# A circular filter over eight tiles folded twice instead of once, in a transformer kernel on one core

## The chip, the cores and the metric

The kernel runs on one core of a Trainium2 chip. Its time is the device time of one execution in microseconds (us), the median of several. The engines are called as the profile calls them: PE is the matmul engine (PEld its weight loads), DVE the vector engine, ACT the scalar engine, POOL the GpSimd engine, SP the queue that issues DMAs.

## The reference

The input is x, float32, 2 batches x 1024 positions x 512 features. Four blocks follow each other, each added to x after a layer norm:

```python
x = x + attn_a(layernorm(x))   # differential attention, 16 heads, causal
x = x + ffn(layernorm(x))      # 8 experts of width 16, the best 2 of them
x = x + attn_b(layernorm(x))   # linear attention with rotary embedding
x = x + ffn(layernorm(x))
```

What matters here is the end of attn_a. Each head gives two causal softmax results, f1 and f2, of the same values. Their difference is filtered along the positions:

```python
attn_freq = (rfft(attn1, axis=1) - lambda_full * rfft(attn2, axis=1)) * filt
attn = irfft(attn_freq, n=1024, axis=1)
attn = attn * rsqrt(mean(attn**2, axis=-1) + eps) * rms_weight * (1 - LAMBDA_INIT)
return attn.reshape(bsz, 1024, 512) @ Wout
```

A fixed factor per frequency is a circular convolution over the 1024 positions. With the positions cut into 8 tiles of 128, output tile i is the sum over j of block[(i - j) mod 8] @ tile j, with eight fixed 128x128 matrices.

attn_b applies a rotary embedding (rope) to the left half of q and of k, sums normalised k times v over the positions, and multiplies q by that sum ahead of W_out.

## The kernel before

**The fold.** A circular convolution over 8 blocks splits into one over 4 blocks of the sums of tiles four apart, and a skew one over 4 blocks of their differences. The kernel stores the 4 sums and 4 differences of a batch in `folded[b]` (8 tiles of 128x512). Four matmuls on the sums give the common part of two output tiles, four on the differences give what separates them; the two tiles are common plus and minus that. TILE (L30) therefore orders the tiles so that the two of a pair follow each other, and that order is the order of the work in stage 2. `filt` holds 11 matrices (L66 to L68), loaded by one DMA.

**Stage 1** is the attention of attn_a: 16 units (batch, quarter of the heads, half of a quarter), each with 9 phases, in one loop of steps (L791). A step handles three phases at once: scores (PE, L461) and exponentials (ACT, L492) of phase `now`, the difference of the two softmax results of phase `last`, and the transposes (L551) of phase `old`. Before the exponentials DVE finds the row minima (L475, L483). The difference is made from a ratio per row: `share` multiplies on POOL (L512), `divide` takes a reciprocal on DVE (L518) and multiplies on POOL (L520), and `join` (L527) on DVE applies the ratio to the 128x1024 weights. The order on PE, DVE, ACT and POOL is written by hand: instructions stand on each engine in program order, and lists named front, small, large, middle, final and rear hang extra work on numbered steps.

At the end of a unit `finish` writes the result, 128 x 8 x 64, on DVE (L607), and `fold` (L615 to L627) makes its sums and differences on POOL: three pairs of an addition and a subtraction, one pair over two tiles and two pairs over one, so two operations of 128 elements a partition and four of 64. It hangs on `rear`, so on POOL it lies between one step's divide and the next step's share. `rotate` (L372, L373) and the scaling of the layer norm are POOL's other work in this stage.

In the last two units the first four tiles of batch 0 (MIXED = 4) are filtered within stage 1. `mix_filter` does eight matmuls 128x256 (L701) for a pair of tiles and half of the columns, `mix_part` (L717) adds and subtracts on POOL, `mix_square` (L721, POOL), `mix_sum` (L725, DVE), `mix_tables` (ACT) and `mix_scale` (POOL) normalise, and `mix_turn` (L742) and `mix_project` (L751) transpose and multiply by Wout. FILTER and TURN say at which step k of the last two units each is done. Wout is scaled by rms_weight on POOL (L816) at k = 11, ahead of that step's share.

**Stage 2** runs over t = 0 to 17, one tile a step for each piece of work, each piece some steps behind the one before. In step t, in the order of the code: `filtered` for the products of tile t + 1 (PE L930, a copy on ACT L939 for the first tile of a pair, a subtraction and an addition on DVE, L941 and L942, for the second), `mixed` (transposes of yn), `head_norm` (square on ACT L947, sum on DVE L949, a reciprocal root by Ln and Exp on ACT L97 and L98 with a step on DVE L103 to L106, and yn on DVE L953), `up` (the experts' second matmul added to x, L1104), `attn_norm` (hn_b on DVE L1125, and three POOL operations on 128x512, L1129 to L1131), `attn_qk` for k and later for q (a bias on DVE L1163, then `rope`), `expert_gate`, `attn_v`, `attn_add`, `projected` and `expert_norm`. From t = 12, when nothing more is to be filtered, `up` and `attn_norm` follow `attn_qk`. From t = 10 the rest of attn_b and the last expert block follow.

`rope` writes two intermediates: ra on DVE (L1148), half of rb on DVE (L1149) and the other half on POOL (L1150), and POOL adds the two (L1151). ra and rb come from a pool with two buffers, one for k and one for q of a tile. In this stage the order is written by hand for PE, DVE and ACT; POOL works in program order.

Of the kernel before, what the change touches and what calls it, by code (L numbers as in the profile page):

```python
# [11 lines left out]
F32 = mybir.dt.float32  # L12
# [6 lines left out]
P = 128  # L19
NB, T, E = 2, 1024, 512  # L20
# [6 lines left out]
NE, NI = 8, 16  # L27
MIXED = 4

TILE = [b * JT + k + h for b in range(NB) for k in range(JT // 2) for h in (0, JT // 2)]  # L30
LAMBDA_INIT = 0.8 - 0.6 * math.exp(-0.3 * 12)
EPS = 1e-5
NEG = -1e30
# [2 lines left out]
def constants():  # L36

    f = np.float32
    t = np.arange(T, dtype=f)

    def tiled(a):
        return np.ascontiguousarray(a.reshape(JT, P, -1).transpose(1, 0, 2).reshape(P, -1))

    inv = (f(1.0) / np.power(f(10000.0), np.arange(0, HD, 2, dtype=f) / f(HD))).astype(f)
    fr = np.outer(t, inv).astype(f)


    r = np.arange(P)
    part = np.where(r // 2 % 2, f(1.0), f(-(HD**-0.5)))[:, None]
    sign = np.where(r % 2, f(1.0), f(-1.0))[:, None]  # L50
    rope_a = np.concatenate([part * np.cos(fr).T[r // 4 % 8], part * sign * np.sin(fr).T[r // 4 % 8]], axis=1).astype(f)

    rot = E // 2
    inv = (f(1.0) / np.power(f(10000.0), np.arange(0, rot, 2, dtype=f) / f(rot))).astype(f)
    fr = (t[:, None] * inv[None, :]).astype(f)
    rope_b = np.concatenate([tiled(np.cos(fr)), tiled(np.sin(fr))], axis=1).astype(f)

    x = np.linspace(0.0, 1.0, T // 2 + 1)  # L60
    taps = np.fft.irfft(np.exp(-0.5 * (x / 0.15) ** 2), n=T)
    lag = (128 * np.arange(JT)[None, :, None] + np.arange(P)[None, None, :] - np.arange(P)[:, None, None]) % T


    block = [taps[lag[:, d]] for d in range(JT)]
    halves = [(block[d] + block[d + 4]) / 2 for d in range(4)]  # L66
    halves += [(block[d % JT] - block[(d + 4) % JT]) / 2 for d in range(-3, 4)]
    filt_k = np.concatenate(halves, axis=1).astype(f)  # L68


    tri = np.tile(np.tril(np.ones((NE, NE), f), -1).reshape(1, -1), (P, 1))
    return {"c_rope_a": rope_a, "c_rope_b": rope_b, "c_filt": filt_k, "c_tri": tri}
# [3 lines left out]
def hybrid_layer_kernel(ctx: ExitStack, tc: tile.TileContext, i: dict, out: bass.AP):  # L76
# [50 lines left out]

    PLACE = [2, 7, 6, 5, 4, 3, 1, 0]

    FOLDED = [0, 1, 2]  # L130
    AT = [0, 1, 3, 2]
    late = ctx.enter_context(ExitStack())
    with ExitStack() as sa:
        keep = sa.enter_context(tc.tile_pool(name="keep", bufs=1))

        folded = [keep.tile([P, JT, E], F32, tag=f"folded{b}", name=f"folded_{b}") for b in range(NB)]
        wrms = keep.tile([P, 1], F32, tag="wrms", name="wrms")
        filt = keep.tile([P, 11, P], F32, tag="filt", name="filt_sb")
        neg_lam = keep.tile([P, 1], F32, tag="neg_lam", name="neg_lam")

        with ExitStack() as sp:
# [65 lines left out]
            def load_others(k):  # L207
                if k == 0:
                    for k in range(4):
                        nc.sync.dma_start(wrms[32 * k : 32 * k + 32, :], i["rms_weight"].rearrange("(p o) -> p o", o=1))  # L210
                elif k == 1:
                    nc.sync.dma_start(wdr, i["w_dr"].rearrange("(c p) f -> p c f", p=P))
                elif k == 2:
                    nc.sync.dma_start(wup, i["w_up"])
                    nc.sync.dma_start(filt, i["c_filt"].rearrange("p (d q) -> p d q", d=11))
                else:
                    nc.vector.tensor_scalar_mul(wrms, wrms, 1.0 - LAMBDA_INIT)

# [396 lines left out]
            def fold(n):  # L615

                b, qt, blk = units[n]
                col = 32 * (4 * qt + 2 * blk)
                r = results.pop(n)

                for to, (low, high, w) in ((2, (5, 0, 2)), (1, (7, 3, 1)), (0, (2, 4, 1))):
                    for op, s in ((nc.gpsimd.tensor_add, 0), (nc.gpsimd.tensor_sub, 4)):
                        op(  # L623
                            folded[b][:, FOLDED[to] + s : FOLDED[to] + s + w, col : col + 64],
                            r[:, low : low + w, :],
                            r[:, high : high + w, :],
                        )  # L627

# [4 lines left out]
            def at(which, t, what, *args):  # L635
                which.setdefault(t, []).append((what, args))
# [54 lines left out]

            mix = {}

            def mix_filter(bank, c0, k, half):
                cols = slice(256 * half, 256 * half + 256)
                y = bank[:, c0 : c0 + 512]
                for d in range(2):
                    for j in range(4):  # L700
                        nc.tensor.matmul(  # L701
                            y[:, 256 * d : 256 * d + 256],
                            filt[:, 4 + k - j + 3 if d else (k - j) % 4, :],
                            folded[0][:, 4 * d + AT[j], cols],
                            start=(j == 0),
                            stop=(j == 3),
                        )
                yield
                sd = mix["sd"] = work.tile([P, 2, 256], F32, tag="sd", name=f"sd_{k}_{half}")
                nc.scalar.copy(sd, y.rearrange("p (d f) -> p d f", d=2))  # L710

            def mix_part(k, half):
                sd = mix.pop("sd")
                for n, op in ((2 * k, nc.gpsimd.tensor_add), (2 * k + 1, nc.gpsimd.tensor_sub)):
                    if half == 0:
                        mix["y", n] = mixy.tile([P, E], F32, tag="y", name=f"y_a{n}", bufs=4)
                    op(mix["y", n][:, 256 * half : 256 * half + 256], sd[:, 0, :], sd[:, 1, :])  # L717

            def mix_square(n):
                sq = mix["sq", n] = work.tile([P, E], F32, tag="sq", name=f"ysq_{n}", bufs=1)  # L720
                nc.gpsimd.tensor_mul(sq, mix["y", n], mix["y", n])  # L721

            def mix_sum(n):
# [31 lines left out]


            FILTER = [5, 8, 9, 10]
            TURN = [13, 14, 17, 18]
            t = (NU - 2) * NP
            for k in range(MIXED // 2):  # L760
                for half in range(2):
                    f = t + FILTER[2 * k + half]
                    at(large, f, mix_filter, 512, k, half)
                    at(middle, f + 1, mix_part, k, half)
                for n in range(2 * k, 2 * k + 2):
                    at(middle, f + 1 + n % 2, mix_square, n)
                    at(rear, f + 2 + n % 2, mix_sum, n)
                    at(front, f + 3 + n % 2, mix_tables, n)
                    at(rear, f + 3 + n % 2, mix_scale, n)
                    at(small, t + TURN[n], mix_turn, n, misc if TURN[n] < 2 * NP else spare)  # L770
                    at(large, t + TURN[n], mix_project, 512, n)

            ordered = {mybir.EngineType.PE, mybir.EngineType.DVE, mybir.EngineType.Activation}
            with tc.manual_schedule(engines=ordered | {mybir.EngineType.Pool}):
# [92 lines left out]
        with ExitStack() as sb:  # L867
# [52 lines left out]

            ys, yns, yTs = {}, {}, {}

            def filtered(n):


                d = n % 2
                b, q = divmod(n // 2, JT // 2)
                y = wide(f"y_{n}")
                for k in range(4):
                    nc.tensor.matmul(  # L930
                        y,
                        filt[:, 4 + q - k + 3 if d else (q - k) % 4, :],
                        folded[b][:, 4 * d + AT[k], :],
                        start=(k == 0),
                        stop=(k == 3),
                    )
                ys[n] = w2k(f"y_{n}", "y", bufs=3)
                if d == 0:
                    nc.scalar.copy(ys[n], y)  # L939
                else:  # L940
                    nc.vector.tensor_sub(ys[n], ys[n - 1], y)  # L941
                    nc.vector.tensor_add(ys[n - 1], ys[n - 1], y)  # L942

            def head_norm(n):
                y = ys.pop(n)
# [195 lines left out]
            def rope(t, j, key):  # L1141
# [2 lines left out]
                cos = rope_b[:, 0, j, :, None].to_broadcast([P, E // 4, 2])  # L1144
                sin = rope_b[:, 1, j, :]
                ra = work.tile([P, E // 4, 2], F32, tag="ra", name=f"ra_{key}")
                rb = work.tile([P, E // 4, 2], F32, tag="rb", name=f"rb_{key}")
                nc.vector.tensor_mul(ra, left, cos)  # L1148
                nc.vector.scalar_tensor_tensor(rb[:, :, 0], left[:, :, 1], -1.0, sin, ALU.mult, ALU.mult)  # L1149
                nc.gpsimd.tensor_mul(rb[:, :, 1], left[:, :, 0], sin)  # L1150
# [69 lines left out]
            with tc.manual_schedule(engines=ordered):  # L1220
                for t in range(NTILE + 2):
# [8 lines left out]
                    if mixing:  # L1230
                        due(expert_back, t - 1, 0, listed=True)
                        if t == 0:
# [4 lines left out]
                            for n in range(2):  # L1237
                                expert_hidden([n], 0)
                            expert_gate([0], 0)

                        for n in range(t + 1 if t else 0, min(t + 2, NTILE - MIXED)):
                            filtered(MIXED + n)
                    turned = MIXED + t - 2 if 0 <= t - 2 < NTILE - MIXED else None
                    if turned is not None:
                        mixed(turned)
                    if 1 <= t <= NTILE - MIXED:
                        head_norm(MIXED + t - 1)
                    if mixing:
                        due(up, t - 1, 0, listed=True)
                        due(attn_norm, t - 1)  # L1250
# [125 lines left out]
```

## Time and profile before

| what | value |
|---|---|
| median of three executions | 1186.89 us (1185.26 to 1187.04) |
| the profiled execution | 1188.05 us |
| its span on the core | 1186.3 us |
| mean granted PE clock | 0.979 |
| stage 1, stage 2 | about 0 to 741 us, 741 to 1186 us |
| PE, DVE, ACT, POOL busy | 1083.5, 950.5, 754.7, 449.0 us |
| fold on POOL (L623) | 96 operations, 1.97 to 1.98 us per unit |
| products of the filter in stage 2 (PE L930) | 96 records for 48 matmuls, 592 ns each |
| products of the filter in stage 1 (PE L701) | 64 records for 32 matmuls, 379 ns each |

Times in the views are microseconds from the start of the span. A line of a timeline or of the chain gives a start, a duration, the engine, the source line and the tile; `x4` says that four instructions are put together. In square brackets stands how long the engine was idle before the instruction, and what ended that. The chain of work that ended last goes back from the last instruction, at each step to what released it. A float32 matmul has two records; records that follow each other overlap, so the time of one is read from a run of them.

### The profile page before, as it was taken

The numbers are of one execution on the slowest core, as the hardware profiler recorded it, in microseconds if no ns is written. First come the engines' busy times: TensorE is split into PE (matmuls) and PEld (weight loads), VectorE is DVE, ScalarE is ACT, GpSimd is POOL, SyncE is SP. The second block draws the span as 40 slices with busy tenths as digits, with TensorE's granted clock in tenths as the row PEclk, the third lists the DMA queues.
The fourth block names the chain that finished last, engine by engine and source line by source line (L and its number), as shares of the span: only waits on it lengthen the run. The fifth ranks groups of instructions, "written<-read, shape, count | busy, mean of one in ns | idle before, by whom it ended". The sixth has DMA issues, their size and how long they took to land.

```text
span 1186.3 us, 23544 instructions
## 1 busy us (share of the span) xinstructions
PE 1083.5 (91%) x8736; PEld 745.6 (63%) x8736; DVE 950.5 (80%) x2025; ACT 754.7 (64%) x1996; POOL 449.0 (38%) x644
## 2 busy tenths in 40 slices
PE   6799999999899999999999977699999989988997
PEld 5577777777677787777777745345454545454554
DVE  4699999989888988998998876578788767747576
ACT  3588988989888888889888855233434332332433
POOL 2335444543433534353354451125344325323300
PEclk9999999999999999999999979799999999989999
DMA  6411211201310110111011602100000000000002
GB/s 208 148 36 56 59 37 51 59 28 41 117 41 15 37 42 15 37 46 37 19 38 41 254 1 86 59 0 1 1 1 0 1 1 1 0 1 36 1 19 88
DMA packets 33346, 52.12 MB, mean 44 GB/s; under 512 B 6481, under 2 KB 11089, under 8 KB 33105
## 3 DMA queue, kind: packets, MB, share of 16 engines
q1 hardware_dynamic: 33232, 50.63, 13.3%
q8 instruction: 69, 1.13, 0.4%
q14 instruction: 45, 0.36, 0.1%
HBM read 23.35 MB, written 6.29 MB: 25 GB/s over the span
## 4 chain that ended last, share of the span: by engine, by line
PE 44%; DVE 32%; ACT 13%; issue 5%; POOL 5%; DMA 1%; SPq 1%; DVEq 0%; POOLq 0%; ACTq 0%
ACT p L492 8%; PE s L461 8%; DVE p L527 7%; DVE least L483 6%; PE bank L329 5%; PE dtp L551 4%; PE py L1215 4%; PE bank L578 3%; PE pq_q L1156 2%; DVE least L475 2%; POOL folded L623 2%; PE hr_f L1031 2%; PE pq_k L1156 2%; PE pq_v L1156 2%; PE y L930 2%
## 5 line engine op out<-in xcount | busy, mean ns | idle before, releaser
L492 ACT ACTIVATE p<-s,least 128x640 f32<-128x640 f32 (+7 forms) x512 | 377.9, 744 | 40.4 <-DVE least L483 24.4
L483 DVE TENSOR_REDUCE least<-s 128x1 f32<-128x896 f32 (+5 forms) x384 | 244.1, 680 | 34.7 <-PE s L461 34.7
L527 DVE SCALAR_TENSOR_TENSOR p<-p,ratio,p 128x1024 f32<-128x1024 f32 (+7 forms) x256 | 233.1, 946 | 9.8 <-POOL ratio L520 8.7
L551 PE MATMUL dtp<-ident,p 128*128 128x128 f32 x1152 | 186.0, 285 | 20.6 <-DVE p L527 9.8
L553 ACT COPY dt<-dtp 128x512 f32<-128x512 f32 x288 | 168.8, 586 | 46.5 <-PE dtp L551 42.9
L461 PE MATMUL s<-keys,qk 32*128 32x128 f32 (+3 forms) x1408 | 169.9, 447 | 3.4 <-DMA keys<-qk 3.4
L551 PEld LDWEIGHTS dtp<-ident,p 128*128 128x128 f32 x1152 | 129.7, 143 | 65.2 <-ACT dt L553 28.1
L475 DVE TENSOR_REDUCE least<-s 128x1 f32<-128x1024 f32 (+1 forms) x96 | 115.8, 1213 | 28.4 <-PE s L461 28.4
L461 PEld LDWEIGHTS s<-keys,qk 32*128 32x128 f32 x1408 | 94.6, 188 | 56.4 <-issue 49.9
L329 PE MATMUL bank<-xnT,wqk 128*128 128x256 f32 x472 | 115.9, 389 | 2.7 <-ACT raw L340 1.8
L520 POOL TENSOR_TENSOR ratio<-ratio,inverse 128x2 f32<-128x2 f32 (+1 forms) x144 | 27.9, 194 | 224.8 <-DVE inverse L518 220.0
L461 PE MATMUL s<-swapped 32*128 32x128 f32 (+2 forms) x896 | 105.6, 347 | 0.0
L512 POOL TENSOR_TENSOR ratio<-sums,neg_lam 128x2 f32<-128x2 f32 (+1 forms) x144 | 69.2, 481 | 95.6 <-ACT p L492 95.6
L492 ACT ACTIVATION_READ_ACCUMULATOR p<-s,least 128x1 f32 x512 | 104.4, 204 | 0.0
L329 PEld LDWEIGHTS bank<-xnT,wqk 128*128 128x128 f32 x472 | 86.1, 193 | 17.6 <-ACT raw L340 5.3
L1129 POOL TENSOR_SCALAR xb_b<-x_sb,mv_b,rr_b 128x512 f32<-128x512 f32 x16 | 37.5, 2343 | 116.2 <-DVE rr_b L106 116.2
L448 PE MATMUL s<-eye 128*128 128x256 bf16 (+1 forms) x320 | 60.9, 251 | 20.2 <-ACT p L492 19.6
L461 PEld LDWEIGHTS s<-swapped 32*128 32x128 f32 x896 | 71.9, 186 | 9.4 <-issue 0.2
L578 PE MATMUL bank<-dt,v 128*32 128x128 f32 x2304 | 69.5, 274 | 0.1
L578 PEld LDWEIGHTS bank<-dt,v 128*32 128x32 f32 x2304 | 60.9, 110 | 5.5 <-issue 3.5
L373 POOL TENSOR_TENSOR other<-other,rope_a_sb 128x512 f32<-128x512 f32 x31 | 64.4, 2076 | 0.0
L1053 ACT ACTIVATE gw_f<-gw_f 128x8 f32<-128x8 f32 (+2 forms) x23 | 4.9, 212 | 93.2 <-DVE gw_f L1049 93.2
(205 smaller groups left out, 1865.7 us busy)
## 6 DMA issues: line engine op xcount, KB each, us to landing
other<-raw SPq DMA_DIRECT2D x64, 128.0 KB, 2.1
xin<-in_query SPq DMA_DIRECT2D x16, 256.0 KB, 2.9
keys<-qk SPq DMA_DIRECT2D x64, 64.0 KB, 1.9
swapped<-qk SPq DMA_DIRECT2D x32, 128.0 KB, 2.3
swapped<-keys SPq DMA_DIRECT2D x32, 128.0 KB, 2.5
x_sb<-in_query SPq DMA_DIRECT2D x16, 256.0 KB, 6.5
out_dram<-x_sb SPq DMA_DIRECT2D x16, 256.0 KB, 2.1
wqk<-in_w_qk SPq DMA_DIRECT2D x8, 256.0 KB, 4.7
```

Of the source, the lines that this page charges most:

```text
L329: nc.tensor.matmul(pp, wqk[:, part, c, :], xnT[b, half][:, c, t0 : t0 + 256], start=(c == 0), stop=(c == EC - 1),)
L373: engine.tensor_mul(other, other, rope_a[:, 1, cols])
L461: nc.tensor.matmul(s[mm][:, c0 : c0 + w], q[r0 : r0 + 32, j * P - back : (j + 1) * P - back], k[r0 : r0 + 32, s0 - back : s0 - back + w], ...
L475: nc.vector.tensor_reduce(least[n][:, e[0] : e[-1] + 1 : e[-1] - e[0] or 1, mm], s[mm].rearrange("p (g k) -> p g k", g=g), AX.X, ALU.min,)
L483: nc.vector.tensor_reduce(least[n][:, e, mm : mm + 1], s[mm][:, c0 : c0 + w], AX.X, ALU.min)
L492: nc.scalar.activation(ps[mm][:, c0 : c0 + w], sv, AF.Exp, bias=low, scale=-1.0, accum_out=sums[n][mm][:, e : e + 1],)
L512: nc.gpsimd.tensor_mul(ratio[:, w], first, neg_lam.to_broadcast([P, w.stop]))
L527: nc.vector.scalar_tensor_tensor(ps[0][:, c0 : c0 + w], ps[1][:, c0 : c0 + w], ratio[:, k : k + 1], ps[0][:, c0 : c0 + w], ALU.mult, ALU.add,)
L551: nc.tensor.transpose(tp[:, k * P : (k + 1) * P], d[:, c0 : c0 + P], ident)
L553: nc.scalar.copy(dt[:, 4 * half : 4 * half + 4, :], tp.rearrange("p (k q) -> p k q", k=4))
L578: nc.tensor.matmul(po[32 * g : 32 * g + 32, c0 : c0 + P], vals[n // 2 % 2][:, k, 64 * (n % 2) + 32 * h : 64 * (n % 2) + 32 * h + 32], dt[: ...
L1156: nc.tensor.matmul(pq, hTs[n][:, c, :], win(c, s), start=(c == 0), stop=(c == EC - 1))
```

## The change

The circular part of the filter is folded again. The sums of tiles four apart are themselves split into sums and differences (tiles two apart), so their part is two products of two matmuls each; the differences of the first fold stay as they were, four matmuls per product. Four output tiles now come from 2 + 2 + 4 + 4 = 12 matmuls where there were 16, in three stages of additions and subtractions. TILE orders the tiles in fours, and `filt` has 12 matrices.

`fold` makes the three subtractions as before, writes the sums in place over `result`, and adds and subtracts these once more: four operations of 128 elements and four of 64. In stage 1 `mix_filter` and `mix_part` work by kind (common or apart) and half, for four tiles at once; the later steps of a tile go by `f + 1 + n // 2`, and TURN is 14, 17, 18, 19. `sd` and `ysq` share a tag with two buffers. In stage 2 `common` and `apart` take the place of `filtered`: products at t = 0 (twice), 1, 3, 4, 5, 7, 8 and 9; the buffers for y are four. `head_norm` stands ahead of them and of `mixed`. In `rope`, rb has one buffer.

```diff
-TILE = [b * JT + k + h for b in range(NB) for k in range(JT // 2) for h in (0, JT // 2)]
+TILE = [b * JT + q + k for b in range(NB) for q in range(2) for k in (0, 4, 2, 6)]
...
+    def sum_products(q, d):
+        if d == 0:
+            return [((q - k) % 2, 1 - k) for k in range(2)]
+        return [(3 + q - k, 3 - k) for k in range(2)]
+
+    def difference_products(q):
+        return [(8 + q - k, 4 + AT[k]) for k in range(4)]
...
-                for to, (low, high, w) in ((2, (5, 0, 2)), (1, (7, 3, 1)), (0, (2, 4, 1))):
-                    for op, s in ((nc.gpsimd.tensor_add, 0), (nc.gpsimd.tensor_sub, 4)):
-                        op(
-                            folded[b][:, FOLDED[to] + s : FOLDED[to] + s + w, col : col + 64],
-                            r[:, low : low + w, :],
-                            r[:, high : high + w, :],
-                        )
+                to = folded[b][:, :, col : col + 64]
+                for k, (low, high, w) in ((2, (5, 0, 2)), (0, (7, 3, 1)), (1, (2, 4, 1))):
+                    r0, r1 = r[:, low : low + w, :], r[:, high : high + w, :]
+                    nc.gpsimd.tensor_sub(to[:, 4 + k : 4 + k + w, :], r0, r1)
+                    nc.gpsimd.tensor_add(r1, r0, r1)
+                nc.gpsimd.tensor_add(to[:, 0:2, :], r[:, 3:5, :], r[:, 0:2, :])
+                nc.gpsimd.tensor_sub(to[:, 2:4, :], r[:, 3:5, :], r[:, 0:2, :])
...
-            def mix_part(k, half):
+            def mix_part(q, half, kind):
                 sd = mix.pop("sd")
...
+                if kind == 0:
+                    nc.gpsimd.tensor_add(y[0], sd[:, 0, :], sd[:, 1, :])
+                    nc.gpsimd.tensor_sub(y[2], sd[:, 0, :], sd[:, 1, :])
+                else:
+                    for d in range(2):
+                        nc.gpsimd.tensor_sub(y[2 * d + 1], y[2 * d], sd[:, d, :])
+                        nc.gpsimd.tensor_add(y[2 * d], y[2 * d], sd[:, d, :])
...
-            TURN = [13, 14, 17, 18]
+            TURN = [14, 17, 18, 19]
...
-            def filtered(n):
...
+            def common(n):
+                b, q = divmod(n // 4, 2)
+                ab = [wide(f"y_{n}_{d}") for d in range(2)]
+                for d in range(2):
+                    products(ab[d], sum_products(q, d), b)
+                for k in (0, 2):
+                    ys[n + k] = w2k(f"y_{n + k}", "y", bufs=4)
+                nc.scalar.copy(ys[n], ab[0])
+                nc.vector.tensor_sub(ys[n + 2], ys[n], ab[1])
+                nc.vector.tensor_add(ys[n], ys[n], ab[1])
+
+            def apart(n):
+                b, q = divmod(n // 4, 2)
+                y = wide(f"y_{n}_2")
+                products(y, difference_products(q + n % 4), b)
+                ys[n + 1] = w2k(f"y_{n + 1}", "y", bufs=4)
+                nc.vector.tensor_sub(ys[n + 1], ys[n], y)
+                nc.vector.tensor_add(ys[n], ys[n], y)
...
-                rb = work.tile([P, E // 4, 2], F32, tag="rb", name=f"rb_{key}")
+                rb = work.tile([P, E // 4, 2], F32, tag="rb", name=f"rb_{key}", bufs=1)
...
-                        for n in range(t + 1 if t else 0, min(t + 2, NTILE - MIXED)):
-                            filtered(MIXED + n)
+                    if 1 <= t <= NTILE - MIXED:
+                        head_norm(MIXED + t - 1)
+                    if mixing:
+                        n = MIXED + t
+                        if t == 0:
+                            common(n)
+                        if t % 4 == 0:
+                            apart(n)
+                        elif t % 4 == 1:
+                            apart(n + 1)
+                        elif t % 4 == 3 and n + 1 < NTILE:
+                            common(n + 1)
                     turned = MIXED + t - 2 if 0 <= t - 2 < NTILE - MIXED else None
                     if turned is not None:
                         mixed(turned)
-                    if 1 <= t <= NTILE - MIXED:
-                        head_norm(MIXED + t - 1)
```

## The prediction

> **What bounds the kernel now.** I read the page's busy row first, then the chain that ended last, first over the span and then in two windows, and then the timelines of the engines that those windows name.
>
> ```profile
> span 1186.3 us, 23544 instructions
> PE 1083.5 (91%) x8736; PEld 745.6 (63%) x8736; DVE 950.5 (80%) x2025; ACT 754.7 (64%) x1996; POOL 449.0 (38%) x644
> ...
> PE 44%; DVE 32%; ACT 13%; issue 5%; POOL 5%; DMA 1%; SPq 1%; DVEq 0%; POOLq 0%; ACTq 0%
> ```
>
> PE is busy for 91% but holds only 44% of the chain, so work taken from PE counts only in the stretches where PE sets the end. POOL, busy 38%, has 5% of the chain, and most of that is the fold. The chain where a unit's fold runs (one of 14 such places):
>
> ```profile
> 606.00 0.50 DVE result L607
> ...
> 606.58 1.24 POOL folded L623 x4
> ...
> 607.95 0.59 POOL folded L623 x2
> 608.55 0.15 POOL ratio L512
> ...
> 608.78 0.20 POOL ratio L520
> ...
> 609.00 3.42 DVE p L527 x2
> ...
> 613.65 1.46 ACT p L492 x4
> ```
>
> The second ratio waits for POOL's queue; the join (L527) starts 0.02 after it, and DVE's minima had ended at 608.95, so nothing else holds the join. In each of the folds of units 0 to 13 the timeline shows this order, with the ratio's end 0.02 to 0.03 after the last minimum and the join right behind. Stage 2, t = 6, DVE's timeline and then POOL's:
>
> ```profile
> 868.13 0.43 DVE L1148 TENSOR_TENSOR ra_q<-qkv_q,rope_b_sb 128x256 f32<-128x256 f32 x1
> 868.47 1.36 DVE L1149 SCALAR_TENSOR_TENSOR rb_q<-qkv_q,rope_b_sb 128x128 f32<-128x128 f32 x1
> 869.75 0.28 DVE L1047 TENSOR_SCALAR sg_f<-hr_f 128x128 f32<-128x128 f32 x1
> ```
> ```profile
> 865.83 2.35 POOL L1129 TENSOR_SCALAR xb_b<-x_sb,mv_b,rr_b 128x512 f32<-128x512 f32 x1 [8.46 <-DVE rr_b L106]
> 868.26 1.42 POOL L1130 TENSOR_TENSOR xb_b<-xb_b,bout_sb 128x512 f32<-128x512 f32 x1
> 869.76 1.27 POOL L1131 TENSOR_TENSOR x_sb<-x_sb,xb_b 128x512 f32<-128x512 f32 x1
> 870.99 0.48 POOL L1150 TENSOR_TENSOR rb_k<-qkv_k,rope_b_sb 128x128 f32<-128x128 f32 x1
> 871.54 0.72 POOL L1151 TENSOR_TENSOR qkv_k<-ra_k,rb_k 128x256 f32<-128x256 f32 x1
> ```
>
> POOL finishes the k rope (872.26) long after DVE wants to begin rb_q (868.47). The chain has rb_q as DVE's link at 826.28, 846.76, 868.55, 889.03, 910.81 and 931.28: from t = 4 to t = 10 DVE sets the step. Its yn (L953) begins at 840.31, 862.11, 882.58, 904.36, 924.83, 946.62: 21.78 us in a step with a y pair (L941, L942), 20.47 in one without. PE's own work is 20.9 a step (773.44 to 794.26 and on to 815.07, the starts of tp_y in the chain), so DVE leads only narrowly; up to t = 3, and again from about 955, PE sets the end.
>
> **The folds.** Six POOL operations of a unit become eight: 2 of 128 elements and 4 of 64 become 4 and 4. By start times in POOL's instructions, a 128-element one takes 0.410 and a 64-element one 0.278 until the next starts (2 x 0.410 + 4 x 0.278 = 1.93; the row of six shows 1.97). New: 4 x 0.410 + 4 x 0.278 = 2.75, so +0.82. [...]
> The three sums now go in place into result, which the subtraction before them reads, and the first of the last two operations reads those sums: the changed kernel's instruction list shows four waits of POOL on itself per fold, and none inside a fold before. The trace has such waits: L1130 begins at 868.26, 0.08 after L1129 ends (868.18), and L1131 0.08 after L1130 (869.68), while fold operations start 0.045 before their predecessor's end. So a wait costs 0.08 + 0.045 = 0.12, four cost 0.48. Bounds: 0 (the wait already met) to 0.58. I take 0.48: **+1.30 a unit**. Behind it in POOL's queue are both ratios, behind those the join, then the next minima, exponentials and scores; the window's edges are all tight, so nothing gives it back. 14 x 1.30 = **+18.2** (11.5 to 19.6). Unit 15's fold (737.8) is followed by no POOL work until 761 and unit 14's is counted with the tail.
>
> **The filter of the first four tiles (stage 1's end).** Matmuls 128x256 fall from 32 to 24, 16 records (8 matmuls) lasting 3.6; PE saves 1.8 at k = 5 and at k = 9 of that tail. mix_part grows from 8 to 12 POOL operations of 0.685 each (+2.7), the squares, sums and scalings of tiles 0 and 1 move a step or so earlier and tile by tile, and the turns and projections go from k = 13, 14, 17, 18 to 14, 17, 18, 19. The place that decides is here:
>
> ```profile
> 687.06 1.72 DVE L527 SCALAR_TENSOR_TENSOR p<-p,ratio,p 128x1024 f32<-128x1024 f32 x1 [4.95 <-POOL ratio L520]
> ```
> ```profile
> 678.02 1.04 POOL L721 TENSOR_TENSOR ysq<-y_a 128x512 f32<-128x512 f32 x1 [2.66 <-DVE yms L725]
> 679.01 1.42 POOL L717 TENSOR_TENSOR y_a<-sd 128x256 f32<-128x256 f32 x2
> 680.41 6.19 POOL L816 TENSOR_SCALAR wout_sb<-wout_sb,wrms 128x512 f32<-128x512 f32 x4
> ```
>
> The scaling of wout stands ahead of the share and the join waits 4.95. With mix_part no longer behind a square that waits 2.66 for DVE, wout starts near 675.7, the join near 682.4: a lead of 4.6. It is spent again: the fold of unit 14 (1.3), later squares, and at k = 19 one turn and projection (3.5 to 3.9 of PE) that now precede weigh and finish. Net **-0.8** (-4 to +3).
>
> **Stage 2's products.** 48 matmuls 128x512 become 36: four, 3.44 us, go at t = 2, 6 and 10. ACT loses three copies of 0.58, DVE gets three more y pairs, of 1.30 to 1.32 (t = 0 twice, then 1, 3, 4, 5, 7, 8, 9, in place of 0, 2, 4, 6, 8, 10). head_norm goes ahead of them on ACT and DVE; its wait for r_m (0.53) stays. At t = 1 the norm need not wait for that step's products, which starts t = 2 about 1 earlier. With the matmuls gone at t = 2, hn_b comes some 5.5 earlier, in the part that PE set.
> At t = 2 and t = 6 PE idles longer. [...] Here PE idled 3.74 ahead of 767.91 and the next eight records took 5.08 instead of 3.45: +1.6. [...]
>
> **rope's rb.** The pool gets one buffer for rb instead of two. So rb_q on DVE waits for POOL's addition that reads rb_k. At t = 6 that is free at 872.26, and rb_q would begin 3.7 after its present start. It then takes about 0.3 in place of 1.36, as it no longer runs beside xb (rb_k at 867.21 took 0.28): the end moves by 2.7. Behind it on DVE stand the gate's operations; the six from ranks to gate take 2.26 beside POOL now (871.17 to 873.43) and took 1.25 at 745.60 with POOL idle, so 1.0 returns. **+1.8 a step** (1.0 to 2.7). In steps from t = 12 POOL is free by then (999.41 to 1000.13 against rb_q at 1000.34); at t = 10 and 11 PE's work covers it.
> Sum: 5.5 less 1.8 at t = 2 leaves a lead of 3.7 to 3.8; sq's wait gone at t = 3 gives 0.6; two more y pairs in t = 3 to 9 than before cost 2.65; seven stalls cost 12.6. Net **+11** (5 to 16). DVE steps are then 22.3 and 23.6, PE's 20.9 or 17.4: PE's saving at t = 6 lies behind DVE.
>
> **Sum.** 18.2 - 0.8 + 11 = 28.4; the profiled execution took 1188.05 (span 1186.3, and 1.75 around it) and would take 1216.4. The median, 1186.89, lies 1.16 lower: **1215 us**.
>
> **Rivals.**
> 1. Faster: PE sets the end and POOL's waits are covered. What is removed counts in full: 12 x 0.86 + 8 x 0.45 = 13.9, giving 1173. For it: PE 91% busy. Against it: the join's start 0.02 after the ratio, and DVE's chain of t = 4 to 10. It decides if a fold adds under 1.0 (14 x 1.0 = 13.9) and rb_q is not held. Chance 0.03.
> 2. The folds cost as said, but rb_q's wait is covered. Stage 2 then gains: -3.8 - 1.8 - 0.6 + 2.65 is -3.5 at most; PE's own 20.9 a step leaves about -2.7. 18.2 - 0.8 - 2.7 = 14.7, giving 1201.6. It needs POOL's chain to end 3.7 sooner. Chance 0.10.
> 3. POOL's waits on itself are free: 11.5 in place of 18.2, giving 1208.5. Chance 0.15.
> 4. All costs at their upper ends: 2.7 a stall (+6.3), half of the clock's 3.3, folds 19.6: giving about 1225. Chance 0.12.
> 5. Gains and losses cancel within 0.2% (what a measurement of this kernel can tell from no change): chance 0.01.
> The forecast itself: 0.59.
>
> **How the numbers follow.** 1215 is the likeliest. The lower ends of all terms (11.5 - 4 + 5) give 1199, the upper ends 1225; cases 2 to 4 and the forecast lie within 1200 to 1226, which keeps room for 2 in 10 outside. Faster 0.03, same 0.01, slower 0.96.
>
> **What would show it.** In the profile after: fold groups of eight with some 3.2 us from the first start to the next ratio, and joins still right behind the ratio (else the first term is wrong); no idle near 5 before the join at k = 11; DVE idle of 3.6 ahead of rb_q, put down to POOL's qkv_k, in t = 2 to 9, and yn spaced 22 to 24. Wrong would be: short waits of POOL on itself, rb_q starting at once, or a join that waits for something other than the ratio.

## The result, and the profile after

The changed kernel takes 1229.91 us (median of four, 1228.99 to 1232.63) against 1186.97 us before: a ratio of 1.0363, with a 95% interval of 1.0336 to 1.0390. That is 43 us more, where 28 were forecast. The profiled execution took 1228.99, its span is 1227.1, and 40.8 us of span are to be placed.

The page of the changed kernel:

```profile
span 1227.1 us, 23506 instructions
PE 1091.0 (89%) x8696; PEld 750.1 (61%) x8696; DVE 939.1 (77%) x2031; ACT 751.6 (61%) x1993; POOL 471.4 (38%) x680
...
PE 38%; DVE 33%; ACT 12%; POOL 9%; issue 6%; DMA 1%; SPq 0%; POOLq 0%; DVEq 0%; ACTq 0%
```

PE has 20 matmuls less to do and is busy for 7.5 us longer: its mean granted clock went from 0.979 to 0.961. POOL's part of the chain went from 5% to 9%.

The simplest way to place the time is to take an instruction that both traces have and to subtract its starts. The table does that for the first operation of a fold and for later marks.

| mark | before | after | shift |
|---|---|---|---|
| fold of unit 0 | 102.36 | 102.38 | +0.0 |
| fold of unit 13 | 647.71 | 664.25 | +16.5 |
| the join's ratio at k = 11 of the tail | 686.84 | 701.10 | +14.3 |
| fold of unit 14 | 697.37 | 712.38 | +15.0 |
| fold of unit 15, the end of stage 1 | 737.76 | 763.34 | +25.6 |
| yn of t = 2 | 777.18 | 797.25 | +20.1 |
| yn of t = 10 | 946.62 | 981.97 | +35.4 |
| yn of t = 12 | 997.02 | 1035.51 | +38.5 |
| end | 1186.3 | 1227.1 | +40.8 |

POOL's timeline where the fold of unit 12 runs (start, duration, engine, line, operation and tile):

```profile
621.15 0.46 POOL L639 TENSOR_TENSOR folded<-result 128x128 f32<-128x128 f32 x1 [2.96 <-DVE result L622]
621.68 0.46 POOL L640 TENSOR_TENSOR result<-result 128x128 f32<-128x128 f32 x1
622.10 0.32 POOL L639 TENSOR_TENSOR folded<-result 128x64 f32<-128x64 f32 x1
622.49 0.32 POOL L640 TENSOR_TENSOR result<-result 128x64 f32<-128x64 f32 x1
...
623.57 0.45 POOL L641 TENSOR_TENSOR folded<-result 128x128 f32<-128x128 f32 x1
623.98 0.45 POOL L642 TENSOR_TENSOR folded<-result 128x128 f32<-128x128 f32 x1
624.39 0.19 POOL L527 TENSOR_TENSOR ratio<-sums,neg_lam 128x2 f32<-128x2 f32 x1
```

The fold takes 3.24 from its first start to the ratio (621.15 to 624.39), against 1.93 before (606.58 to 608.51). The operation behind a wait on POOL itself starts 0.53 after a 128-element operation and 0.39 after a 64-element one, where 0.410 and 0.278 were enough without it: 0.11 to 0.12 a wait, as forecast.

The chain behind that fold, in order of time (start, duration, what):

```profile
624.66 0.20 POOL ratio L535
624.87 0.02 issue
624.89 2.01 DVE p L542
626.90 0.14 issue
627.04 1.06 PE dtp L566 x4
628.10 3.05 PE bank L593 x64
```

The last line is new. These 64 small matmuls take 1.95 to 1.96 by PE's timeline in the kernel before (1.95 at 611.71, with a granted clock of 1.00 from 606 to 616). The join came later and left PE idle for 1.82 ahead of 627.04, and the granted clock between 628 and 631 is 0.59. Stage 2 at t = 6, DVE:

```profile
877.54 0.29 DVE L1180 SCALAR_TENSOR_TENSOR rb_q<-qkv_q,rope_b_sb 128x128 f32<-128x128 f32 x1 [3.73 <-POOL qkv_k L1182]
```

rb_q is held for 3.73 by POOL's qkv_k. This stands in each step from t = 3 to t = 9 and at t = 11; at t = 2 and t = 10 it is 1.15.

### The profile page after: what moved, and what is told of

Its sections match the earlier page's. It is cut to its first block, busy times and chain, and to the rows that moved or that the text cites. A ratio compares the mean times of both kernels' runs of the same rounds, so it can differ in the third digit from the quotient of the medians.

```text
span 1227.1 us, 23506 instructions
## 1 busy us (share of the span) xinstructions
PE 1091.0 (89%) x8696; PEld 750.1 (61%) x8696; DVE 939.1 (77%) x2031; ACT 751.6 (61%) x1993; POOL 471.4 (38%) x680
## 3 DMA queue, kind: packets, MB, share of 16 engines
q1 hardware_dynamic: 33232, 50.70, 12.8%
## 4 chain that ended last, share of the span: by engine, by line
PE 38%; DVE 33%; ACT 12%; POOL 9%; issue 6%; DMA 1%; SPq 0%; POOLq 0%; DVEq 0%; ACTq 0%
DVE least L498 9%; ACT p L507 7%; PE s L476 7%; DVE p L542 7%; PE bank L344 4%; PE dtp L566 4%; PE py L1246 4%; PE bank L593 3%; PE pq_q L1187 2%; DVE least L490 2%; POOL xb_b L1160 2%; PE hr_f L1062 2%; PE po_f L1132 2%; PE pq_k L1187 1%; PE y L950 1%
## 5 line engine op out<-in xcount | busy, mean ns | idle before, releaser
L593 PE MATMUL bank<-dt,v 128*32 128x128 f32 x2304 | 74.7, 287 | 0.1
L593 PEld LDWEIGHTS bank<-dt,v 128*32 128x32 f32 x2304 | 65.3, 115 | 7.0 <-issue 5.3
```

Source lines behind the costliest of these rows:

```text
L593: nc.tensor.matmul(po[32 * g : 32 * g + 32, c0 : c0 + P], vals[n // 2 % 2][:, k, 64 * (n % 2) + 32 * h : 64 * (n % 2) + 32 * h + 32], dt[: ...
```

## The experiments

Two accounts stood against each other at the start. By the first, the forecast's terms are right and only their sizes are off. By the second, the end of stage 1, which was counted at -0.8, is where the missing time went, and the one buffer for rb also counts behind t = 10. The first four kernels take the change apart.

### One part at a time

**e1_rb2**: the changed kernel with rb's second buffer back.

```diff
-                rb = work.tile([P, E // 4, 2], F32, tag="rb", name=f"rb_{key}", bufs=1)
+                rb = work.tile([P, E // 4, 2], F32, tag="rb", name=f"rb_{key}")
...
-                rank = stat.tile([P, g, NE], F32, tag=f"rank_{g}", name=f"rank_{key}")
+                rank = stat.tile([P, g, NE], F32, tag=f"rank_{g}", name=f"rank_{key}", bufs=1 if g == 4 else 4)
```

> The changed kernel with two buffers for rope's rb again (the space comes from one tag of small rank tiles, used once). If the one buffer costs what the trace of the changed kernel suggests (1.66 us in each of the steps t = 2 to 9, and the loss of 5.5 us between t = 10 and t = 12 comes from rb_q's wait too), the time falls from 1230 to about 1212. If the loss after t = 10 has another cause, 1217. If the wait for POOL only takes the place of another wait, it stays at 1230.

Measured: 1215.67 us, ratio to before 1.0226 (1.0208 to 1.0244). Against the changed kernel's 1.0363 that is 1.37% of 1187, some 16 us (14 by the medians, 12.8 by the two traces). It is nearer to the second expectation, 1217, than to the first: by the traces, stage 2 up to the yn of t = 10 is 12.2 shorter with two buffers, but 3.5 of the 5.4 lost behind it stay, 2.4 of them at t = 10.

**e2_rb1**: the same part alone, on the kernel before.

```diff
-                rb = work.tile([P, E // 4, 2], F32, tag="rb", name=f"rb_{key}")
+                rb = work.tile([P, E // 4, 2], F32, tag="rb", name=f"rb_{key}", bufs=1)
```

> The kernel before with one buffer for rb and nothing else changed. By the prediction's step of 1.8 us a step over the DVE-bound steps t = 3 to 9: 1187 + 12.6 = 1199.5. If t = 11 adds its 3.7 us: 1203. If the wait is covered: 1187.

Measured: 1205.72 us, ratio 1.0141 (1.0122 to 1.0160), +16.7. The two directions agree within their intervals: the one buffer costs some 16 us. In its trace yn falls back by 1.61 to 1.78 a step from t = 4 on, with a single 3.5 at t = 7: there PE idles 2.26 ahead of 882.75, and the granted clock from 884.0 to 887.4 is 0.50.

**e3_fold8**: the kernel before with the eight-operation fold.

```diff
-                for to, (low, high, w) in ((2, (5, 0, 2)), (1, (7, 3, 1)), (0, (2, 4, 1))):
-                    for op, s in ((nc.gpsimd.tensor_add, 0), (nc.gpsimd.tensor_sub, 4)):
...
+                for k, (low, high, w) in ((2, (5, 0, 2)), (0, (7, 3, 1)), (1, (2, 4, 1))):
+                    r0, r1 = r[:, low : low + w, :], r[:, high : high + w, :]
+                    nc.gpsimd.tensor_sub(to[:, 4 + k : 4 + k + w, :], r0, r1)
+                    nc.gpsimd.tensor_add(r1, r0, r1)
+                nc.gpsimd.tensor_add(to[:, 0:2, :], r[:, 3:5, :], r[:, 0:2, :])
+                nc.gpsimd.tensor_sub(to[:, 2:4, :], r[:, 3:5, :], r[:, 0:2, :])
```

> The kernel before with the fold of eight operations alone (the filter then reads sums of another order, so the output is not the reference's; the work is the same). By the prediction 14 x 1.30 = 18.2: 1205. If POOL's waits on itself cost nothing: 1198.5. If the fold is covered: 1187.

Measured: 1209.89 us, ratio 1.0179 (1.0160 to 1.0197), +21. From one unit to the next the shift against the kernel before grows by 1.29 to 1.31 in six of fourteen units, by 1.91 to 1.97 in five, and by 0.2 to 1.16 in three early ones, where the traces of kernels with the same stage 1 also differ, by up to 2.4. In one of the five (unit 6) the chain of e3_fold8 has the slow matmuls again:

```profile
365.03 0.20 POOL ratio L520
365.23 0.03 issue
365.26 2.00 DVE p L527
367.26 0.14 issue
367.40 0.63 PE dtp L551 x4
368.03 3.49 PE bank L578 x64
```

PE had been idle for 1.81 ahead of 367.40, and the granted clock from 368.0 to 371.4 is 0.52; at the same place the kernel before idles 0.51, keeps 1.00 and has its 64 matmuls in 1.96 by PE's timeline (3.56 in e3_fold8). So the fold's own 1.30 is as forecast, and the clock adds 0.6 to 0.66 in five units.

**e4_tail**: the kernel before with the changed filter of the first four tiles.

```diff
-            def mix_filter(bank, c0, k, half):
+            def mix_filter(bank, c0, q, half, kind):
...
-            TURN = [13, 14, 17, 18]
+            TURN = [14, 17, 18, 19]
...
+            for n in range(MIXED):
+                at(middle, f + 1 + n // 2, mix_square, n)
+                at(rear, f + 2 + n // 2, mix_sum, n)
+                at(front, f + 3 + n // 2, mix_tables, n)
+                at(rear, f + 3 + n // 2, mix_scale, n)
```

> The kernel before with the changed filter of the first four tiles at the end of stage 1 alone (24 matmuls, 12 operations of mix_part, the later turns; the fold and stage 2 are those of before, so the output is not the reference's). By the prediction -0.8 us: 1186. By the trace of the changed kernel, where the tail lost 7.7 us, 1.3 of them the fold of unit 14: about +6.5, 1193.5.

Measured: 1194.71 us, ratio 1.0046 (1.0030 to 1.0062), +5.5 to 6.5: the second account. What the forecast saw is there, and is lost again: the ratio of k = 11 comes 4.2 earlier than in the kernel before, and the fold of unit 15 then comes 6.5 later.

### What the tail loses

**e5_turn** moves only the turns and projections.

```diff
-            TURN = [13, 14, 17, 18]
+            TURN = [14, 17, 18, 19]
```

> The kernel before with the turns and projections of the first four tiles at k = 14, 17, 18, 19 in place of 13, 14, 17, 18, and nothing else. If at k = 13 they run in the shadow of POOL's chain to the ratio and at k = 19 on the path (turn and projection took 3.5 to 3.9 us of PE there): +3.5, 1191. If PE's work at k = 13 was on the path as much as at k = 19: 1187.

Measured: 1194.71 us, ratio 1.0055 (1.0036 to 1.0074), +6.5, twice what was expected. Of its 6.2 us in the trace up to unit 15's fold, 3.5 come at k = 19, as expected. The other 2.7 come at k = 14 and 15: with no projection at k = 13 PE has gaps of 0.74 to 1.73 one after the other, and the projection at k = 14 takes 6.05 (eight records) against 4.33 and 3.69 for those at k = 13 and 14 of the kernel before.

**e6_spread** is e4_tail with the scalings one in a step.

```diff
-                at(front, f + 3 + n // 2, mix_tables, n)
-                at(rear, f + 3 + n // 2, mix_scale, n)
+                at(front, f + 3 + n, mix_tables, n)
+                at(rear, f + 3 + n, mix_scale, n)
```

> The tail of e4_tail with the scalings of the four tiles (tables and mix_scale) one in a step, at k = 13, 14, 15, 16, in place of two at k = 13 and two at k = 14. If the two scalings ahead of the minima of k = 15 are what made that step 5.6 us longer, 2 to 4 us of the 6.5 come back: about 1191. If it is the projections' place, it stays near 1194.

Measured: 1187.18 us, ratio 0.9997 (0.9984 to 1.0009): the tail's whole loss is gone, more than expected. DVE's timeline of e4_tail shows the place, at k = 14:

```profile
708.51 0.69 DVE L774 TENSOR_TENSOR x_sb<-x_sb,bank 128x512 f32<-128x512 f32 x1 [3.89 <-PE bank L772]
...
710.12 0.17 DVE L104 SCALAR_TENSOR_TENSOR rt_y<-yms,r_y 128x16 f32<-128x16 f32 x1
...
710.33 1.04 DVE L105 TENSOR_TENSOR rt_y<-rt_y,r_y 128x16 f32<-128x16 f32 x1
...
711.68 1.04 DVE L105 TENSOR_TENSOR rt_f<-rt_f,r_f 128x1 f32<-128x1 f32 x1
```

And POOL's:

```profile
710.29 1.05 POOL L757 TENSOR_TENSOR y_a<-y_a,rr_y 128x512 f32<-128x512 f32 x1 [7.84 <-DVE rt_y L104]
711.65 1.05 POOL L757 TENSOR_TENSOR y_a<-y_a,rr_y 128x512 f32<-128x512 f32 x1 [0.32 <-DVE rt_f L104]
```

The 16-element operation L105 lasts 1.04 where it lasts 0.16 for the first tile (at 709.84): behind the first tile's step POOL begins its scaling of 512 elements, and the second tile's step stands beside it and ends with it (711.37, POOL's 711.34). The scaling of the second tile then meets L105 of the next layer norm (rt_f) in the same way. Two tiles in one step make these collisions; with one in a step L105 takes 0.16 to 0.18 throughout. The same happens at k = 13 (L105 at 697.65, 1.04), and behind it PE has the projection in 5.69, against 3.70 in e6_spread; the granted clock from 703 to 718 is 0.84 in e4_tail and 1.00 in e6_spread. The three collisions add 2.6 on DVE and the projection 2.0 on PE; how the whole loss divides between the two was not separated. The engines of e4_tail and then of e6_spread by windows (bounds, length, busy of PE, PEld, DVE, ACT, POOL, granted clock, DMA share, GB/s):

```profile
690.00:703.00 13.00, 7.78 (x43) 5.72 (x42) 11.80 (x27) 7.12 (x22) 6.74 (x14) 0.50 0.01 2
703.00:718.00 15.00, 12.23 (x121) 6.84 (x120) 10.57 (x25) 7.17 (x24) 3.12 (x5) 0.84 0.00 1
```
```profile
690.00:703.00 13.00, 10.19 (x48) 6.61 (x48) 10.96 (x24) 9.15 (x27) 5.67 (x13) 0.66 0.00 1
703.00:718.00 15.00, 11.74 (x153) 8.41 (x152) 14.17 (x36) 11.14 (x33) 4.17 (x9) 1.00 0.12 20
```

With the scalings spread, the ratio of k = 11 comes 4.2 earlier as in e4_tail, and this lead is what pays for k = 19.

### What stage 2's products are worth

**e9_stage2**: the kernel before with the changed stage 2 (and two buffers for rb).

```diff
-            def filtered(n):
+            def common(n):
...
+            def apart(n):
...
-                        for n in range(t + 1 if t else 0, min(t + 2, NTILE - MIXED)):
-                            filtered(MIXED + n)
+                    if 1 <= t <= NTILE - MIXED:
+                        head_norm(MIXED + t - 1)
```

> The changed stage 2 alone (36 products in place of 48, head_norm ahead of them) with two buffers for rb, on the fold and the tail of the kernel before (so the filter reads sums of another order and the output is not the reference's; the room for rb comes from two tags of small tiles, used once each). By the prediction's working without the stalls: -2.7, 1185. By the trace of e1_rb2 from unit 15's fold to the end: -0.8, 1187. If the removed matmuls count in full, 12 x 0.86 = 10.3: 1177.

Measured: 1190.83 us, ratio 1.0004 (0.9988 to 1.0020): nothing. By the marks 5.2 us are won by t = 2 (5.5 forecast); 4.2 of them are gone at the yn of t = 10, 2.65 by the two additional y pairs, while the rest lies at t = 3 and 4 and its cause stays open; and 1.7 more go at t = 10. There the removed product leaves PE idle for 4.20, and the records of py behind it take 8.73. In the seven traces with stage 2 as before the idle there is 2.71 to 2.76 and py takes 7.03 in each; in the four with the changed stage 2 and two buffers for rb (e1_rb2, e8_after_late, e9_stage2, e10_late_spread) it is 4.20 to 4.21 and py takes 8.48 to 8.73.

**e12_warm** puts four matmuls back at that one place, with their result unused.

```diff
+                    if t == 10:
+                        products(wide("warm"), difference_products(0), 1)
                     turned = MIXED + t - 2 if 0 <= t - 2 < NTILE - MIXED else None
```

> e9_stage2 with four matmuls 128x512 put back at t = 10, at the place where the kernel before had that step's product, their result unused (the output is as wrong as that of e9_stage2). There PE idled 4.20 us and the sixteen records of py then took 8.73 us in place of 7.03 in the kernel before. If the idle is what halves the clock: py takes 7.0 to 7.4 us, the granted clock of that stretch is 1.0, and the run is 1.7 us shorter although PE does 3.44 us more. If the half clock has another cause: py stays at 8.7 and the time is the same or up to 3 us longer.

Measured: 1191.50 us, ratio 1.0018 (1.0007 to 1.0029). PE's timeline of e9_stage2 and then of e12_warm:

```profile
952.57 1.24 PE L1054 MATMUL hr_f<-wdr_sb,xT_f 128*128 128x136 f32 x8 [4.20 <-ACT xT_f L1041]
953.61 8.73 PE L1238 MATMUL py<-ws,QT 128*128 128x512 f32 x16
```
```profile
938.11 3.60 PE L942 MATMUL warm<-folded,filt_sb 128*128 128x512 f32 x8
...
952.91 1.19 PE L1054 MATMUL hr_f<-wdr_sb,xT_f 128*128 128x136 f32 x8 [1.76 <-ACT xT_f L1041]
953.94 7.03 PE L1238 MATMUL py<-ws,QT 128*128 128x512 f32 x16
```

The step does what was expected: 3.44 us of useless matmuls make py 1.70 shorter, the clock of 950 to 956 is 1.00 in place of 0.80, and the shift of yn between t = 10 and t = 11 is 1.7 smaller. So the idle is what halves the clock there: 4.20 of it did, 1.76 did not. The run as a whole is not shorter, though, and the ratios speak against the 1.7 that was expected. By the traces 2.5 are lost again behind the yn of t = 12, 0.8 of them near 1050 and 1.7 at 1173, where the granted clock is 0.50 from 1172.5 to 1175.9 and 1.00 in e9_stage2. e4_tail and e6_spread, whose stage 2 is the same, differ by 3.3 in that part, so it stays open whether the four matmuls have to do with it.

### Putting the losses right

**e7_foldlate**: the kernel before with the folds two steps later, behind that step's ratio.

```diff
-                at(rear, t + NP + 4 - (n >= NU - 2), fold, n)
+                if n < NU - 1:
+                    at(middle, t + NP + 6, fold, n)
+                else:
+                    at(rear, t + NP + 3, fold, n)
```

> The kernel before with the folds of units 0 to 14 two steps later, behind POOL's second ratio of that step, where POOL is idle. In the kernel before the ratio ends within 0.03 us of DVE's last minimum, so the fold just fits and nothing is gained: 1187. If the fold's whole 1.97 us was on the path, 14 x 1.97 = 27.6: about 1160.

Measured: 1177.32 us, ratio 0.9908 (0.9889 to 0.9927): faster than the kernel before by 10.5, and neither expectation. Each of the units 7 to 13 gains 0.86 to 0.88. The join follows DVE's last minimum as before, but the ratio is done by then, and POOL's rotation behind it (L372, 1.27 long) starts 0.8 ahead of the join, at 598.10, where it started 0.1 ahead of it (608.92). So the join stands beside 0.47 of it in place of 1.19. The chain of e7_foldlate at unit 12:

```profile
597.81 1.19 DVE least L483 x2
598.99 2.61 DVE p L527 x2
```

The join takes 2.61 in place of 3.42 in the chain. By DVE's timeline it is 0.72 shorter (2.70, from 598.91), as much as it stands less beside L372, and starts 0.13 earlier against the minima. No run moves the rotation alone, so that the overlap is the cause is read from the trace only.

**e8_after_late** is the same edit on e1_rb2.

> The changed kernel with two buffers for rb (as e1_rb2) and the folds of units 0 to 14 two steps later. If the growth of the fold is what stage 1 lost, 18 to 21 us go from e1_rb2's 1215.7: about 1196. If the eight operations delay POOL's work two steps later in the same way, 1215.

Measured: 1184.36 us, ratio 0.9970 (0.9958 to 0.9983), some 30 us below e1_rb2, where 18 to 21 were expected: on top of the fold's growth it has the 0.87 a unit that e7_foldlate showed. Its units are as fast as those of e7_foldlate: behind the ratio, 3.24 us of fold are as good as 1.93.

**e10_late_spread** adds the spread scalings of e6_spread to e8_after_late.

> e8_after_late with the scalings of the first four tiles one in a step as in e6_spread: the changed kernel without its three losses. If the tail's loss adds to the others: 1184.4 - 6.6 = 1178. If it was part of the fold's: 1184.

Measured: 1180.28 us, ratio 0.9908 (0.9879 to 0.9937). Against e8_after_late the ratio falls by 0.62%, some 7 us (4 by the medians), so the tail's loss adds to the others, as in the first expectation. The changed arithmetic without its three losses is where the old arithmetic is with its fold moved: the removed matmuls gain nothing.

**e11_wout**: e7_foldlate with wout scaled in four parts.

```diff
-                    if t == (NU - 1) * NP + 2:
-                        for c in range(EC):
-                            nc.gpsimd.tensor_scalar_mul(wout[:, c, :], wout[:, c, :], wrms)
...
+                    if (NU - 1) * NP <= t < (NU - 1) * NP + 4:
+                        c = t - (NU - 1) * NP
+                        nc.gpsimd.tensor_scalar_mul(wout[:, c, :], wout[:, c, :], wrms)
                     do(middle, t)
```

> e7_foldlate with the scaling of wout in four parts, one behind the ratio of each of the steps k = 9 to 12, in place of all four ahead of the share of k = 11. If the join's wait of 4.95 us and the half clock behind it are on the path: 4 to 6 us less than 1177.3, about 1172. If POOL's work then delays the squares as much: 1177.

Measured: 1176.79 us, ratio 0.9872 (0.9833 to 0.9911). In the trace the ratio of k = 11 comes 5.8 earlier against its own stage and the end 5.2 earlier than that of e7_foldlate, but the trace is of the fastest of four runs that spread from 1170.86 to 1179.00, and the intervals of the two overlap. So it has the lowest median here, but a gain over e7_foldlate is not shown. It leaves the filter as it was.

## Why the prediction was wrong

The parts, each alone on the kernel before, add up to the whole within the intervals: 1.41 (rb) + 1.79 (fold) + 0.46 (tail) + 0.04 (stage 2) = 3.70%, and the change has 3.63%. The direction was right; the time, 1215, was 15 short and outside the range of 1200 to 1226. By the traces the forecast is 12.4 short (40.8 against 28.4): the tail accounts for 8.6 and stage 2 from t = 10 for 5.4, while the other two rows are 1.6 too high.

| step of the forecast | forecast | measured |
|---|---|---|
| folds of units 0 to 13 | +18.2 | +16.5 over units 0 to 12 in the changed kernel (1.27 each); the fold alone, to the end, +21 |
| the tail of stage 1, unit 14's fold in it | -0.8 | 25.6 - 16.5 - 1.3 = +7.8 |
| stage 2 up to t = 10 | +11 | 35.4 - 25.6 = +9.8 |
| stage 2 from t = 10 | 0 | 40.8 - 35.4 = +5.4 |

**The folds** were right in mechanism and nearly in size: 0.82 for the operations and 0.48 for four waits is what the trace shows. Two things around it were not. The claim that nothing but the ratio holds the join was true only in its last 0.02 us: with the fold out of the way a unit gains 0.87 (e7_foldlate), 0.72 of it because the join is shorter and only 0.13 because it starts earlier. And the clock adds 0.66 in some units. That the mean is 1.27 is partly luck: in the changed kernel seven units have 1.29 to 1.31, three with a granted clock of 0.50 behind the gap 1.96 to 1.97, and three early ones 0.2 to 0.7. Of the readings, the fold has 25.8 of POOL's 59.7 us in the chain, the largest part but not most of it.

**The tail** is the step that failed first: "a lead of 4.6. It is spent again". The lead came nearly as worked out, 4.2 in e4_tail and e6_spread. One turn and projection at k = 19 costs 3.5, as forecast, and in e6_spread the two about cancel (ratio 0.9997). The term that is missing is two scalings in a step: the forecast saw them as tiles moving "a step or so earlier", put nothing down for them, and they cost 6 to 7 by e6_spread against e4_tail. In the trace the loss shows as DVE's operations beside POOL's scaling (1.04 each) and as PE's lower granted clock (0.50 and 0.84 in the two windows, against 0.66 and 1.00).

**The stall of rb_q** had the right instruction, the right releaser and the right length (3.7 forecast, 3.72 and 3.73 measured), the net of 1.8 a step is 1.66 to 1.78 up to t = 10, the steps of 22.3 and 23.6 are 22.13 and 23.45, and the 12.6 for seven stalls is 12.2 by the traces of the changed kernel and e1_rb2. "At t = 10 and 11 PE's work covers it" is the step that failed: t = 11 stalls for 3.72. In the kernel before, the chain there was PE's alone; in the changed kernel it runs (start, duration, what):

```profile
1021.28 0.73 POOL qkv_k L1182
...
1022.03 0.29 DVE rb_q L1180
...
1035.30 0.66 PE tp_f L930 x4
1035.95 5.13 PE pq_q L1187 x8
```

DVE and ACT come late behind the stall, PE idles 3.04 ahead of 1035.30, and its pq_q then takes 5.13 in place of 3.44, with a granted clock of 0.50 from 1036.7 to 1040.1. Alone, on the kernel before, the buffer costs 16.7 in place of 12.6, and the clock is in that too: 1.8 at t = 7, and at t = 10 py takes 8.57 in place of 7.03.

**The products** were worth 2.7 to 3.5 without the stalls by the working of rival 2, and nothing by e9_stage2. The failed step is the clock's, for which the sum puts nothing down. At t = 2 and 6 nothing was lost: in e9_stage2 the clock is 1.00 from 773 to 952. But at t = 10, where the forecast put down no idle, 4.20 of it stand ahead of py, for which DVE waits, and py takes 8.73 there, 1.70 more than behind 1.76 of idle in e12_warm. No run shows the clock's 3.3, of which rival 4 and the upper end of the range have a half: it was the author's estimate, the 1.6 read at 767.91 put down twice, and the runs showed 0 at t = 2 and 6 and 1.70 at t = 10. Nor was that reading clean: the granted clock there was 0.50 from 761.3 to 771.5, and that began within an idle of 6.65 that came before the 3.74.

The misses have one thing in common: a delay was priced at its own length, and what PE does behind it at full clock. Rival 4, the upper ends with half of the clock's 3.3, was the nearest in number (1225), but by larger stalls and folds, which is not where the time went.

## What to carry to other kernels

A pool's buffer count in a diff is a wait: look up who reads the last buffer, and where that reader stands in its own queue. When work is taken from PE, whose granted clock fell behind idles here (0.52 behind 1.81 us in e3_fold8; py 8.73 in place of 7.03 behind 4.20 in e9_stage2), price the idle that it leaves, by the first matmuls behind it and not by its length; and when two small steps are put into one, ask which of them will run beside another engine's long operation (1.04 in place of 0.16 for L105 of e4_tail). Work that has a reader far away, like these folds, belongs behind the small operations that others wait for, not ahead of them.

## What the runs showed of the hardware

PE's granted clock fell to one half behind short idles: in e3_fold8 a gap of 1.81 us was followed by a stretch of 3.4 us at 0.52 (368.0 to 371.4), in which 64 matmuls took 3.56 by PE's timeline in place of 1.96, while behind 0.51 at the same place of the kernel before it stayed at 1.00.

Which gaps do it can be read from the changed kernel's trace. The changes of its granted clock lie on one grid of 3.41 us (412.03, 415.44, 541.74, 545.15, 627.07, 630.48 and so on). In each of the units 6 to 13 PE idles 1.81 to 1.87 at this place. In units 7, 10, 12 and 13 the gap lies inside one interval of the grid, and the clock is 0.50 in the next: in unit 7 the gap is 409.52 to 411.33, the interval 408.62 to 412.03, and the 64 matmuls take 3.56. In units 6, 8 and 9 an edge of the grid divides the gap (454.80 to 456.61 in unit 8, the edge at 456.41), the clock stays at 1.00, and the 64 matmuls take 1.95. It also stays at 1.00 behind the gaps of 1.57 to 1.65 in units 1 to 4, each inside one interval. One gap inside an interval does not do it: in unit 11, 1.82 that begin 0.08 behind an edge (582.78, the edge at 582.70) leave the clock at 1.00.

A 16-element operation of DVE took 1.04 us beside a POOL operation of 1.05 in e4_tail (at 710.33), against 0.16 just before (709.84), and one of a single element took 1.04 in the same way (711.68). The changed kernel has three such cases, at 718.15, 730.12 and 731.48, 1.04 each. In all five the operation ended 0.02 to 0.03 behind POOL's, so it lasted as long as the operation beside it, whatever its own size.
